# Two tables of places for a Mamba pipeline's work, laid anew, with a ninth buffer of h

## The chip, the core and the metric

One core of a Trainium2 chip runs the whole kernel in one launch. Every number is fp32. The metric is the device time of one execution in microseconds (us), the median of the runs.

## The reference

Four layers run one after the other on an image of 2 x 64 channels of 96 x 96 points. Layer 0 is attention over all 9216 points of a batch. Layer 3 is a 3 x 3 convolution whose taps come from the image's mean. The change concerns layers 1 and 2, which are Mamba blocks: a normalised input goes through a projection to 128 channels and a gate, a causal convolution of 4 taps, SiLU, and then a scan over the sequence with 16 states a channel:

```python
dt = softplus(dt_proj(x_proj(xc)[:4]) + dt_b)       # per channel and position
h  = exp(dt * A) * h + dt * B * xc                  # 128 channels x 16 states
y  = sum over states of h * C
out = out_proj((y + xc * D) * silu(gate))
```

Layer 1 scans the 9216 points of each batch as one sequence, so that its state is carried on. Layer 2 runs four such blocks, with RMS norms: forwards and backwards along the image's columns, then forwards and backwards along its rows. Its sequences are 96 long and start from nothing.

## The kernel before, in words

The Mamba work is cut into units of 768 positions: 24 in layer 1 (12 chunks of each batch) and 96 in layer 2 (8 sequences of 96, in pairs that share one normed input, one forwards, one backwards). A unit is 16 steps of 128 x 768: two halves of the positions (384 each), in each half two parts of eight states, in each part four steps of two blocks of 16 channels.

What one step does, and on which engine:

- `read` (L946): SP starts two transfers, which spread a block's rows of dt and of dt * xc from DRAM over 128 partitions. Six `spread` buffers hold them.
- `room` (L961) takes a buffer of h, of which there are `HELD` (8, L710), used in turn.
- `decay` (L967): ScalarE writes exp(dt * A), two activations of 384 columns (L973), into the h buffer.
- `shared` (L975): every fourth step TensorE makes B for four steps in one PSUM bank (L978). It must not overwrite a B that is still read.
- `inputs` (L984): VectorE multiplies the spread by B (L986) for two steps at a time, into the two PSUM tiles `place`.
- `scan` (L988): VectorE scans 768 columns (L1000; in layer 1 two scans of 384, L995) from decay and inputs into h. Then GpSimd multiplies h by C (L1002), which is called product below. In layer 1 it first copies the carried state (L996).
- `gather` (L1004): TensorE sums the products of a step into y (L1013), two steps at a time. After it the h buffer is free.

In some steps, the "asides" (`ASIDES`, L1154), the two operands change sides: GpSimd makes the inputs, into an SBUF tile `bx`, from a copy of B that ScalarE makes (`b_copy`, L980, line L982), and ScalarE puts the decay into `place`. Layer 1 has one aside a unit, at step 5; layer 2 has two, at steps 3 and 10, with a copy of B for each.

Beside the steps, parts of other units are done. The head of a unit runs two to three units ahead: the norm (`norm_centre` to `norm_affine`, L771 to L826; in layer 2 `image_0` and `image_1`, L790 and L795, copy the image and square it for both units of a pair), `conv` on TensorE (L830) and `conv_read` on ScalarE (L850), `gate_mm` and `gate_read`, `silu` (L859, with a table load before and after it), `step_mm` and `step_read` (L875, L876), `step_exp`, `step_log`, the sums on TensorE (`sum_mm`, L897) and `sum_read` (L902), `step_u` on GpSimd (L906), `step_write` on SP (L914), and `c_mm` with `c_read` (L920, L924) for C, twice. The end of a unit is done while the next one runs: `y_half` and `y_read` (L1017, L1020) take y from PSUM, `y_gate` (L1023) multiplies it by the gate on GpSimd, `tail_0` and `tail_1` (L1029) project it, and `tail_read` (L1043) writes the image. The matmuls' results of all these go through one PSUM tile, `mm`, so each waits for the reader of the one before. `other` prepares the next weights.

What sets the order: each of these has a place, a number of steps, in one of two tables, `CARRY` for layer 1 (L1056) and `FRESH` for layer 2 (L1104). `events` (L1160) adds the step's number to it, `run` (L1197) adds 16 for each unit and sorts everything of all units by place. In that order the instructions go into the queues of their engines. Each engine works its queue in order, and semaphores hold an instruction until what it needs is there. So a place matters only through the order that it gives on each engine.

Two rules of the built program are seen in the trace. Readers of one PSUM bank on two engines are ordered as well: where `b_copy` stands ahead of the inputs that read the same B, VectorE's instruction waits for ScalarE's copy. And `y_half` and `y_read` hold the first matmul of the next half of y.

Of the kernel before, what the change touches and what calls it, by code (L numbers as in the profile page):

```python
# [692 lines left out]
class Mamba:  # L693
# [13 lines left out]


    STEPS = 16
    HELD = 8  # L710
    BX = 1
    SPREADS = 6
    YG = 2
# [247 lines left out]
    def room(self, u, step):  # L961
        u.h[step] = self.by_half(self.work("h", bufs=self.HELD))
        u.decay[step], u.bx[step] = u.h[step], self.place(step)
        if step in self.aside(u):
            u.decay[step], u.bx[step] = self.place(step), self.by_half(self.work("bx", bufs=self.BX))
# [77 lines left out]
    def tail_read(self, u):  # L1043
# [10 lines left out]


    CARRY = dict(  # L1056
        norm_centre=-47.1,
        norm_square=-46.9,
        image_0=-37.15,
        image_1=-31.05,  # L1060
        norm_mean=-34.35,
        norm_root=-34.15,
        norm_scale=-32.6,
        norm_affine=-30.6,
        conv=-27.35,
        conv_read=-26.9,
        gate_mm=-26.15,
        gate_read=-24.85,
        silu=-24.6,
        step_mm=-23.9,  # L1070
        step_read=-23.1,
        step_exp=-22.05,
        step_log=-20.6,
        sum_mm_0=-20.23,
        sum_mm_1=-20.01,
        sum_read=-19.0,
        step_u=-12.65,
        step_write=-9.55,
        c_mm_0=-1.35,
        c_read_0=-0.05,  # L1080
        c_mm_1=1.65,
        c_read_1=2.45,
        y_half=11.97,
        y_read=18.72,
        y_gate=19.35,
        tail_0=25.55,
        tail_1=25.6,
        tail_read=26.05,
        other_0=2.77,
        other_1=4.25,  # L1090
        decay=-2.25,
        aside_decay=-0.75,
        aside=-1.7,
        inputs=0.0,
        scan=0.7,
        gather=3.65,
        shared=-1.8,
        read_0=-7.35,
        read_1=-3.25,
        read_2=-1.6,  # L1100
        read_3=0.5,
        b_copy_0=2.7,
    )
    FRESH = dict(  # L1104
        norm_centre=-47.0,
        norm_square=-41.9,
        image_0=-41.3,
        image_1=-36.9,
        norm_mean=-34.9,
        norm_root=-34.3,  # L1110
        norm_scale=-32.35,
        norm_affine=-30.75,
        conv=-27.35,
        conv_read=-26.4,
        gate_mm=-26.25,
        gate_read=-25.85,
        silu=-25.8,
        step_mm=-25.05,
        step_read=-24.5,
        step_exp=-22.6,  # L1120
        step_log=-21.4,
        sum_mm_0=-21.28,
        sum_mm_1=-21.16,
        sum_read=-19.5,
        step_u=-13.25,
        step_write=-9.35,
        c_mm_0=-1.5,
        c_read_0=-0.55,
        c_mm_1=1.65,
        c_read_1=2.75,  # L1130
        y_half=11.12,
        y_read=18.42,
        y_gate=18.65,
        tail_0=23.7,
        tail_1=24.6,
        tail_read=25.8,
        other_0=0.42,
        other_1=1.5,
        decay=-3.2,
        aside_decay=-1.15,  # L1140
        aside=-2.65,
        inputs=0.3,
        scan=0.7,
        gather=2.95,
        shared=-1.55,
        read_0=-8.2,
        read_1=-8.15,
        read_2=-5.7,
        read_3=-0.55,
        b_copy_0=-1.2,  # L1150
        b_copy_1=6.55,
    )
    TABLES = (CARRY, FRESH)
    ASIDES = ((5,), (3, 10))  # L1154
    CORE = ("decay", "aside_decay", "aside", "inputs", "scan", "gather", "shared", "read", "b_copy", "other")

    def aside(self, u):
        return self.ASIDES[bool(u.carry is None)]

# [422 lines left out]
```

## Time and profile before

| | us |
|---|---|
| median of 3 runs (lowest, highest) | 7484.11 (7477.61, 7490.45) |
| the profiled execution | 7481.5 |
| its span, first to last instruction | 7479.7 |
| layer 0 and the start of layer 1 (to 2553.5 us) | 2553.5 |
| layer 1 after its start (to 3569) | 1015.5 |
| layer 2 (to 7420) | 3851 |
| layer 3 | 59.7 |

Busy time in layer 2, as shares of its 3851 us: VectorE 97%, GpSimd 91%, ScalarE 84%, TensorE 77%. The granted TensorE clock was 0.93 on average there and 0.90 in layer 1.

Mean durations of the groups that the text uses, over the whole execution:

| line, engine | shape | count | mean ns |
|---|---|---|---|
| L1000 VectorE, scan | 128 x 768 | 1344 | 1736 |
| L1000 VectorE, scan in aside form | 128 x 768 | 192 | 1740 |
| L986 VectorE, inputs | 128 x 768 | 1704 | 948 |
| L1002 GpSimd, product | 128 x 768 | 1920 | 1818 |
| L986 GpSimd, aside's inputs | 128 x 768 | 216 | 1816 |
| L973 ScalarE, half a decay into h | 128 x 384 | 2688 | 607 |
| L982 ScalarE, copy of B | 128 x 384 | 216 | 469 |
| L859 ScalarE, SiLU | 128 x 1536 | 120 | 1483 |

How to read it: instructions of one engine overlap by about 0.1 us, so a pair takes less than twice the mean. An engine's idle time is put down to the instruction that ended last of those it waited for. What the kernel's time depends on is the idle time of the busiest engine in each stage, so a wait of another engine counts only as far as it reaches that one.

### The profile page before, as it was taken

Reading aid. Unit: us, or ns where it says so; the run is one execution under the profiler, and the core shown is the slowest. Engines: PE = TensorE matmul, PEld = TensorE weight load, DVE = VectorE, ACT = ScalarE, POOL = GpSimd, SP = SyncE. Lnnn points to the kernel's source line nnn. Section 1 sums busy time; section 2 is a strip of 40 time slices with the busy share of each in tenths; the row PEclk is TensorE's granted clock in tenths of the full one; section 3 lists DMA queues with packets and bytes.
Section 4 is the critical chain, followed back from the end, with each engine's and each line's share of the span. In section 5 each row is a group of like instructions: output and inputs, shape, how many; then the busy total and the mean of one; then the engine's idle time right before and its main releaser. Section 6 shows DMA issues by size and latency. Waiting matters only on the chain. (4 is left out here: it accounts for less than half of the span.)

```text
span 7479.7 us, 106202 instructions
## 1 busy us (share of the span) xinstructions
PE 6309.8 (84%) x38502; PEld 2338.3 (31%) x38502; DVE 6739.8 (90%) x5732; ACT 5470.8 (73%) x7876; POOL 4609.8 (62%) x3074
## 2 busy tenths in 40 slices
PE   9999999999998788787777777777777777777777
PEld 3333333333332232222222222222233233322322
DVE  6778877888886699999999999999999999999999
ACT  5555555555554687787888888888888888888884
POOL 0000000000000588888899898889999999999996
PEclk9999999999998799888999899989999999999998
DMA  1000000000000566566667666666667666666774
GB/s 46 1 1 1 1 1 1 3 5 5 6 6 29 129 167 156 150 168 155 169 175 184 165 180 169 175 168 181 178 174 183 178 179 180 175 180 177 180 183 127
DMA packets 301157, 878.12 MB, mean 117 GB/s; under 512 B 33608, under 2 KB 35660, under 8 KB 300112
## 3 DMA queue, kind: packets, MB, share of 16 engines
q1 hardware_dynamic: 300184, 869.94, 44.9%
q8 instruction: 304, 4.98, 0.3%
q14 instruction: 229, 1.88, 0.1%
q10 hardware_dynamic: 440, 1.32, 0.1%
HBM read 767.71 MB, written 103.42 MB: 116 GB/s over the span
## 5 line engine op out<-in xcount | busy, mean ns | idle before, releaser
L1002 POOL TENSOR_TENSOR h<-h,C 128x768 f32<-128x768 f32 x1920 | 3454.6, 1818 | 364.8 <-DVE h L1000 308.5
L1000 DVE TENSOR_TENSOR_SCAN h<-h,place 128x768 f32<-128x768 f32 x1344 | 2288.2, 1736 | 12.6
L313 ACT ACTIVATE e<-f_exp 128x1024 f32<-128x1024 f32 x1296 | 1257.7, 1022 | 986.8 <-PE f_exp L299 986.8
L986 DVE TENSOR_TENSOR place<-spread,B 128x768 f32<-128x768 f32 x1704 | 1548.2, 948 | 214.4 <-ACT xa L982 78.9
L973 ACT ACTIVATE h<-spread,xa 128x384 f32<-128x384 f32 x2688 | 1459.9, 607 | 80.9 <-PE y L1013 56.1
L324 PE MATMUL y<-e,xb 64*64 64x512 f32 x10368 | 1232.1, 590 | 0.0
L299 PE MATMUL f_exp<-theta,phi 64*64 64x512 f32 x10368 | 1229.9, 589 | 2.0 <-DVE xb L284 1.5
L1013 PE MATMUL y<-h,held 128*32 128x384 f32 x7680 | 1041.1, 532 | 212.3 <-POOL h L1002 212.3
L402 DVE TENSOR_TENSOR acc_e<-acc_e,e 128x1024 f32<-128x1024 f32 x612 | 771.7, 1261 | 300.9 <-ACT e L313 282.7
L338 POOL TENSOR_TENSOR ys<-ys,y_one 128x512 f32<-128x512 f32 x36 | 45.9, 1274 | 1456.8 <-DVE ys L337 1456.8
L411 DVE TENSOR_TENSOR acc_e<-acc_e,e 128x1024 f32<-128x1024 f32 x612 | 810.9, 1325 | 65.9 <-DVE acc_e L402 2.8
L978 PE MATMUL B<-raw,xa 128*128 128x384 f32 x960 | 497.6, 604 | 323.1 <-DVE place L986 310.4
L995 DVE TENSOR_TENSOR_SCAN h<-h,state,place 128x384 f32<-128x384 f32 x720 | 671.4, 992 | 1.7 <-PE y L1013 0.5
L324 PEld LDWEIGHTS y<-e,xb 64*64 64x64 f32 x10368 | 393.6, 133 | 728.2 <-issue 722.4
L299 PEld LDWEIGHTS f_exp<-theta,phi 64*64 64x64 f32 x10368 | 395.5, 133 | 715.0 <-issue 703.0
L363 POOL TENSOR_TENSOR xa<-xa,t_att 64x512 f32<-64x512 f32 x36 | 55.0, 1527 | 755.8 <-ACT t_att L361 735.2
L920 PE MATMUL mm<-raw,xa 128*128 128x384 f32 x960 | 386.4, 527 | 138.4 <-ACT C L924 78.2
L1013 PEld LDWEIGHTS y<-h,held 128*32 128x32 f32 x7680 | 198.7, 111 | 933.9 <-POOL h L1002 516.7
L743 PE MATMUL mm<-dtu,ident 128*128 128x384 f32 x960 | 418.2, 541 | 9.6 <-ACT xb L1048 4.9
L973 ACT ACTIVATE h<-spread,rates 128x384 f32<-128x384 f32 x720 | 394.9, 605 | 31.1 <-PE y L1013 16.8
L986 POOL TENSOR_TENSOR bx<-spread,xa 128x768 f32<-128x768 f32 x216 | 392.3, 1816 | 14.0 <-ACT xa L982 13.2
L973 ACT ACTIVATE place<-spread,xa 128x384 f32<-128x384 f32 x384 | 224.0, 583 | 199.8 <-DVE h L1000 193.3
(229 smaller groups left out, 7385.9 us busy)
## 6 DMA issues: line engine op xcount, KB each, us to landing
spread<-rows SPq DMA_DIRECT2D x1920, 384.0 KB, 6.1
rows<-dtu SPq DMA_DIRECT2D x120, 768.0 KB, 4.8
image<-pre SPq DMA_DIRECT2D x11, 384.0 KB, 2.3
xb<-image SPq DMA_DIRECT2D x11, 384.0 KB, 8.7
xa<-in_x SPq DMA_DIRECT2D x1, 2304.0 KB, 22.0
xa<-in_x SPq DMA_DIRECT2D x3, 384.0 KB, 11.5
xb<-in_x SPq DMA_DIRECT2D x3, 384.0 KB, 12.3
xa<-in_x SPq DMA_DIRECT2D x1, 1152.0 KB, 18.2
```

What stands on the lines that cost most here:

```text
L299: nc.tensor.matmul(f[rows_of(half), bass.ts(side, NB)], lhsT=phi[at, m * P + half * C : m * P + (half + 1) * C], rhs=theta[at, bass.ts(i, ...
L313: nc.scalar.activation(e, f, AF.Exp)
L324: nc.tensor.matmul(ys[half][rows_of(side)], lhsT=g[at, m, :], rhs=e[at, bass.ts(side, NB)], start=m < 2, stop=m >= KEYS - 2,)
L402: nc.vector.tensor_add(block.acc, block.acc, es[0])
L411: nc.vector.tensor_add(block.acc, block.acc, es[1])
L973: self.nc.scalar.activation(u.decay[step][:, q], dt[:, q], AF.Exp, scale=rate)
L978: self.nc.tensor.matmul(self.B, lhsT=u.w.bc[0][part], rhs=x, start=True, stop=True)
L986: engine.tensor_mul(u.bx[step], self.spread(u, step, 1), B)
L995: nc.vector.tensor_tensor_scan(h[:, q], decay[:, q], bx[:, q], state[:, q : q + 1], ALU.mult, ALU.add)
L1000: nc.vector.tensor_tensor_scan(*flat, 0.0, ALU.mult, ALU.add)
L1002: nc.gpsimd.tensor_mul(h, h, C)
L1013: self.nc.tensor.matmul(y, lhsT=self.t.gather[block // 4], rhs=u.h[step][:, q], start=False, stop=stop)
```

## The change

`HELD` goes from 8 to 9. Layer 1's aside goes from step 5 to step 3. Nearly all numbers of both tables are set anew. The code that uses them is the same. The diff, cut to the entries that alter an engine's order or that the text speaks of (layer 1 first):

```diff
-    HELD = 8
+    HELD = 9
...
     CARRY = dict(
...
-        norm_square=-46.9,
+        norm_square=-47.15,
...
-        norm_affine=-30.6,
+        norm_affine=-31.35,
...
-        gate_read=-24.85,
-        silu=-24.6,
-        step_mm=-23.9,
-        step_read=-23.1,
-        step_exp=-22.05,
-        step_log=-20.6,
+        gate_read=-25.25,
+        silu=-25.05,
+        step_mm=-24.7,
+        step_read=-23.55,
+        step_exp=-22.1,
+        step_log=-21.0,
...
-        step_u=-12.65,
-        step_write=-9.55,
-        c_mm_0=-1.35,
-        c_read_0=-0.05,
+        step_u=-12.15,
+        step_write=-8.3,
+        c_mm_0=-1.0,
+        c_read_0=0.05,
...
-        aside_decay=-0.75,
-        aside=-1.7,
+        aside_decay=-0.85,
+        aside=-1.8,
...
-        b_copy_0=2.7,
+        b_copy_0=0.2,
     )
     FRESH = dict(
...
-        norm_root=-34.3,
+        norm_root=-33.5,
...
-        step_log=-21.4,
+        step_log=-21.2,
...
-        c_read_0=-0.55,
-        c_mm_1=1.65,
+        c_read_0=-0.7,
+        c_mm_1=2.15,
...
-        y_half=11.12,
-        y_read=18.42,
-        y_gate=18.65,
-        tail_0=23.7,
-        tail_1=24.6,
+        y_half=10.72,
+        y_read=18.17,
+        y_gate=18.7,
+        tail_0=24.35,
+        tail_1=25.55,
...
-        decay=-3.2,
-        aside_decay=-1.15,
-        aside=-2.65,
-        inputs=0.3,
-        scan=0.7,
-        gather=2.95,
+        decay=-2.7,
+        aside_decay=-0.55,
+        aside=-2.3,
+        inputs=-0.05,
+        scan=0.8,
+        gather=3.05,
...
-        b_copy_0=-1.2,
-        b_copy_1=6.55,
+        b_copy_0=-1.05,
+        b_copy_1=7.45,
     )
-    ASIDES = ((5,), (3, 10))
+    ASIDES = ((3,), (3, 10))
```

Sorted within a unit's 16 steps, the queues of layer 2 differ in these places: on TensorE `c_mm_1` comes behind the gathers of steps 14 and 15 of the unit before, and `tail_0` behind those of steps 4 and 5; on ScalarE `c_read_0` comes ahead of decay 2, `y_read` ahead of decay 5, `y_half` ahead of `step_log` (it was behind `image_1`), and decay 1 ahead of `norm_root`. In layer 1, on ScalarE, `c_read_0`, `b_copy` and `norm_affine` open the unit, ahead of `norm_square`; decay 3 is an aside and decay 5 is not; `gate_read` comes ahead of decay 9 and `step_read` ahead of decay 11. On GpSimd the aside's inputs come behind product 0 (they were behind product 2), `y_gate` behind product 2 and `step_u` behind product 3. On TensorE `c_mm_0` comes behind the gathers of steps 10 and 11, and `norm_centre` ahead of those of steps 12 and 13.

More of the change, by code (lines that the diff above doesn't have):

```diff
@@ L1056 @@
     CARRY = dict(
-        norm_centre=-47.1,
-        norm_square=-46.9,
-        image_0=-37.15,
-        image_1=-31.05,
-        norm_mean=-34.35,
+        norm_centre=-47.35,
+        norm_square=-47.15,
+        image_0=-36.75,
+        image_1=-31.65,
+        norm_mean=-34.45,
         norm_root=-34.15,
         norm_scale=-32.6,
-        norm_affine=-30.6,
+        norm_affine=-31.35,
         conv=-27.35,
-        conv_read=-26.9,
-        gate_mm=-26.15,
-        gate_read=-24.85,
-        silu=-24.6,
-        step_mm=-23.9,
-        step_read=-23.1,
-        step_exp=-22.05,
-        step_log=-20.6,
-        sum_mm_0=-20.23,
-        sum_mm_1=-20.01,
-        sum_read=-19.0,
-        step_u=-12.65,
-        step_write=-9.55,
-        c_mm_0=-1.35,
-        c_read_0=-0.05,
-        c_mm_1=1.65,
+        conv_read=-27.15,
+        gate_mm=-26.45,
+        gate_read=-25.25,
[4 more added lines that the diff above has]
+        step_log=-21.0,
+        sum_mm_0=-20.63,
+        sum_mm_1=-20.21,
+        sum_read=-18.5,
+        step_u=-12.15,
+        step_write=-8.3,
+        c_mm_0=-1.0,
+        c_read_0=0.05,
+        c_mm_1=1.75,
         c_read_1=2.45,
@@ L1084 @@
         y_read=18.72,
-        y_gate=19.35,
-        tail_0=25.55,
+        y_gate=19.1,
+        tail_0=24.9,
         tail_1=25.6,
         tail_read=26.05,
-        other_0=2.77,
-        other_1=4.25,
+        other_0=2.87,
+        other_1=3.25,
         decay=-2.25,
-        aside_decay=-0.75,
-        aside=-1.7,
+        aside_decay=-0.85,
+        aside=-1.8,
         inputs=0.0,
@@ L1097 @@
         shared=-1.8,
-        read_0=-7.35,
+        read_0=-7.25,
         read_1=-3.25,
-        read_2=-1.6,
-        read_3=0.5,
-        b_copy_0=2.7,
+        read_2=-2.7,
+        read_3=0.35,
+        b_copy_0=0.2,
     )
     FRESH = dict(
[L1105 to L1109, printed above, removed]
-        norm_root=-34.3,
[L1111 to L1120, printed above, removed]
-        step_log=-21.4,
[L1122 to L1127, printed above, removed]
-        c_read_0=-0.55,
-        c_mm_1=1.65,
-        c_read_1=2.75,
-        y_half=11.12,
-        y_read=18.42,
-        y_gate=18.65,
-        tail_0=23.7,
-        tail_1=24.6,
@@ L1136 @@
-        tail_read=25.8,
-        other_0=0.42,
-        other_1=1.5,
-        decay=-3.2,
-        aside_decay=-1.15,
-        aside=-2.65,
-        inputs=0.3,
-        scan=0.7,
-        gather=2.95,
-        shared=-1.55,
[L1146 to L1149, printed above, removed]
-        b_copy_0=-1.2,
-        b_copy_1=6.55,
+        norm_centre=-46.85,
+        norm_square=-45.6,
+        image_0=-40.4,
+        image_1=-36.35,
+        norm_mean=-34.45,
+        norm_root=-33.5,
@@ new lines @@
+        norm_scale=-32.95,
+        norm_affine=-32.8,
+        conv=-27.2,
+        conv_read=-26.1,
+        gate_mm=-26.0,
+        gate_read=-25.6,
+        silu=-25.5,
+        step_mm=-25.25,
+        step_read=-23.75,
+        step_exp=-22.4,
+        step_log=-21.2,
+        sum_mm_0=-21.18,
+        sum_mm_1=-20.76,
+        sum_read=-19.0,
+        step_u=-12.6,
+        step_write=-10.75,
+        c_mm_0=-1.2,
+        c_read_0=-0.7,
+        c_mm_1=2.15,
+        c_read_1=2.85,
+        y_half=10.72,
@@ L1152 @@
+        y_read=18.17,
+        y_gate=18.7,
+        tail_0=24.35,
+        tail_1=25.55,
+        tail_read=25.8,
+        other_0=0.72,
+        other_1=0.4,
+        decay=-2.7,
[4 more added lines that the diff above has]
+        gather=3.05,
+        shared=-1.55,
+        read_0=-7.2,
+        read_1=-6.3,
+        read_2=-4.1,
+        read_3=-1.2,
+        b_copy_0=-1.05,
+        b_copy_1=7.45,
     )
     TABLES = (CARRY, FRESH)
-    ASIDES = ((5,), (3, 10))
+    ASIDES = ((3,), (3, 10))
```

## The prediction

> **What bounds the kernel now.** I read the engine totals, then the busy time by stage, then the waits of the long stage, then the timelines of single units.
>
> In the windows below (columns: stretch, its length, then busy us and count of PE, PEld, DVE, ACT, POOL, granted clock, DMA share, GB/s) the first row is layer 1 after its start, the second layer 2:
>
> ```profile
> 2553.50:3569.00 1015.50, 819.10 (x3210) 297.14 (x3208) 977.70 (x1101) 808.70 (x1251) 864.44 (x838) 0.90 0.63 160
> 3569.00:7420.00 3851.00, 2964.59 (x12626) 1131.00 (x12626) 3743.59 (x2920) 3230.13 (x5073) 3495.47 (x2059) 0.93 0.68 176
> ```
>
> VectorE is the bound: idle 37.8 us in layer 1 and 107.4 us in layer 2. No reordering can gain more than these 145 us. Layer 2 has 96 units of 16 steps, so it loses 1.12 us a unit. The waits between 4150 and 7300 us (78.5 units; us, times, longest) say to what:
>
> ```profile
> PE B L978 <- DVE place L986: 210.8, 145, 2.9
> PE y L1013 <- POOL h L1002: 156.2, 112, 2.7
> ACT raw L850 <- PE conv L845: 114.3, 72, 2.7
> DVE place L986 <- ACT xa L982: 64.8, 79, 1.9
> ACT h L973 <- PE y L1013: 45.8, 67, 1.0
> ```
>
> Only the fourth row is VectorE's: once a unit the inputs of step 0 or step 8 wait for ScalarE's copy of B (L982). The other rows show what makes that copy late. The timeline of two units, on three engines (start, us, engine, line, operation; in brackets the idle time before it and what ended it):
>
> ```profile
> 5243.10 0.91 PE L978 MATMUL B<-raw,xa 128*128 128x384 f32 x2 [1.97 <-DVE place L986]
> 5245.51 2.81 PE L845 MATMUL conv<-xn,xa 64*128 64x384 f32 x16
> ...
> 5260.75 0.84 PE L1013 MATMUL y<-h,held 128*32 128x384 f32 x4 [2.70 <-POOL h L1002]
> ...
> 5271.86 0.80 ACT L902 COPY dtu<-mm 128x768 f32<-128x768 f32 x1 [0.70 <-PE mm L743]
> 5273.34 1.12 ACT L973 ACTIVATE h<-spread,xa 128x384 f32<-128x384 f32 x2 [0.68 <-PE y L1013]
> ...
> 5277.52 1.83 DVE L986 TENSOR_TENSOR place<-spread,B 128x768 f32<-128x768 f32 x2 [1.56 <-ACT xa L982]
> ...
> 5322.35 0.91 PE L978 MATMUL B<-raw,xa 128*128 128x384 f32 x2 [2.13 <-DVE place L986]
> 5325.87 3.29 PE L845 MATMUL conv<-xn,xa 64*128 64x384 f32 x16
> ...
> 5336.60 1.83 DVE L986 TENSOR_TENSOR place<-spread,B 128x768 f32<-128x768 f32 x2 [0.74 <-ACT xa L982]
> ```
>
> After a pause of 2.13 us TensorE runs its convolution slowly; the convolution's reader, SiLU and the copy of B follow it in ScalarE's queue, and VectorE waits 0.74 us. After 1.97 us the convolution was fast and that wait is missing, but a second pause (2.70 us, for GpSimd's products) slows the sums, and the next copy is 1.56 us late. From 5196.67 to 5357.13 us (four units) VectorE waits 0.69 + 0.92 + 0.40 + 1.56 + 0.74 + 0.32 = 4.63 us. A unit without a wait takes 5277.52 - 1.56 - 5237.06 = 38.90 us.
>
> [...] The trace agrees: slow spells begin near 5203.5 and 5323.0 us[...]. It also shows the same 1.97 us pause both with and without a spell (5202.71 and 5243.10), so phase matters. [...] Here VectorE's reading at 5277.52 starts 0.03 us after ScalarE's copy of the same B ends, so a late copy holds VectorE though it needs nothing from it. [...] The scans stay at 1736 and 1740 ns whether the aside form or not, so moving the aside step changes no duration.
>
> **The change part by part.** The tables' figures act through the sort alone, so I sorted both tables and compared each engine's queue. In layer 2, VectorE's, GpSimd's and SP's queues are the same as before but for two small weight-preparing places; "half a step later" moves decays past nothing except the few entries named here.
>
> Ninth h buffer: decay 0 no longer needs the gathers of step 8 to be done. That removes the 0.68 us wait (45.8/67). It lies on the chain to step 0's copy only in the unit of each pair with the norm (every second unit), where the copy then ends near 5276.8 instead of 5277.5: 0.7 us.
>
> The second C product behind gathers 14 and 15 (they stood the other way round): gather 15 needs GpSimd's product of step 15, which ended 2.14 us after the start of the next unit's inputs (5239.20 against 5237.06). Then come gathers 0.85 and C product 1.5, done at +4.5 us; the inputs of step 2 end at +6.0 and release B for step 4. The pause is 1.5 us instead of 1.97 to 2.92[...], and the pause ahead of the gathers is 1.2 to 1.75. All lie under the 1.97 us that began a spell only sometimes, so I expect the convolution fast in nearly all units. It then ends 1.8 us after the start of the inputs of step 4 (5248.32 against 5246.50), not 3.4 (5329.16 against 5325.75). From its reader to the end of the copy for step 8 ScalarE needs 7.3 us, 9.2 in all, and the inputs of step 8 start at 10.0: the waits of 0.92, 0.74 and, following from them, 0.40 and 0.32 go. The 0.69 shrinks to 0.15, since from the reader to the next copy ScalarE has 27.7 us of work.
>
> What is late next: GpSimd's order is unchanged, so its pause of 2.5 to 2.7 us ahead of gathers 6 and 7 stays, and the sums stay slow: 0.70 (sum_read) + 0.15 = 0.85 us in every second unit, 48 x 0.85 = 41 us. Gain 107 - 41 = 66; I take 62, for units whose spell remains. Bounds: 100 us if the sums' spell goes too (48 x 0.15 remain), 17 us if the convolution stays slow as often as now (24 x 0.7).
>
> First tail half behind gathers 4 and 5: fills 0.85 of TensorE's 1.83 us wait for step_read; nothing on VectorE's path. Copy of C ahead of decay 2, y_read ahead of decay 5, y_half ahead of step_log, decay 1 ahead of the norm's root: nothing, covered by ScalarE's 1.45 us wait for scan 1 (place, 5242.22 and 5282.68). y_half delays step_log by 0.46 us, under the 0.7 us wait of sum_read at worst: up to 0.46 x 48 = 22 us if it isn't hidden.
>
> Layer 1, step_read ahead of decay 11: the inputs of step 12 wait for PE B once in most units, 25.1 us in 13 waits, because B stands behind the tails, which stand behind step_read:
>
> ```profile
> 3001.43 0.86 PE L743 MATMUL mm<-yg,mats 128*64 128x384 f32 x2 [2.68 <-ACT dtu L876]
> ...
> 3008.17 1.83 DVE L986 TENSOR_TENSOR place<-spread,B 128x768 f32<-128x768 f32 x2 [1.52 <-PE B L978]
> ```
>
> One decay (two activations) is 1.03 us: 13 x 1.03 = 13 us. At most all 25 go.
>
> Layer 1, aside at step 3 (GpSimd's product behind product 0, ahead of 1; step_u behind product 3): from the end of scan 14 GpSimd needs 9.6 us to have it (wait-free from product 14 on), VectorE reaches scan 3 after 10.0. The decay, now behind the copies of C and B, norm_affine, norm_square and decay 4, ends 8.4 us after the unit's start by my count, against 8.2. I take 1 us lost in all; bounds 0 and 24 x 0.5 = 12 us. The copy of B now waits for VectorE's inputs 0 and 1 (done at +1.8; ScalarE gets there at about +3): nothing. step_write follows step_u 1.25 steps later, at 7.7 of the unit's 16, and SP's reads keep their order behind it: with 4.8 us for the write and 6.1 for a spread (the page's medians; a step is 2.7 us) the next unit's first spread lands near 11.8, and its first decay comes at 13.75: nothing; without that cover each us late costs 24.
>
> Sum: 62 + 13 - 1 = 74 us off the profiled execution (span 7479.7, execution 7481.5): 7407.5. The median of the runs is 2.6 above that execution, so 7410.
>
> **The rivals.** *Phase decides (A):* [...] Then only the ninth buffer pays: 17 + 12 us, 7484 - 29 = 7455. For it: 1.97 us did and didn't trip. [...]
>
> *New wait (B), slower:* y_read now stands ahead of decay 5 and of step 3's decay, and waits for gather 15, so GpSimd's lag reaches VectorE's scan 3. With product 15 done at +L, that decay ends at L + 0.9 + 0.45 + 1.03 + 1.15 = L + 3.5; scan 3 starts at +7.8. At today's L of 2.14 there are 2.1 us to spare. From L = 4.3 each us costs 96 us; from 5.1 it outweighs the gain, and L = 5.3 gives about 7504. Against: GpSimd waits for scans 12 to 14 (1.45 us before each pair), so its lag is wiped out each unit.
>
> *Nothing happens (C):* ScalarE's chain is simply full, and removed waits reappear at the same copy: 7480. Against: it waits 114 us for the convolution, which shortens.
>
> **How the numbers follow.** Forecast 0.58 (7372 to 7440: the gain of 100 in layer 2 with 12 in layer 1 at the low end; y_half's 22 us and half of layer 1's 12 lost at the high end: 7438). A 0.20 (7440 to 7466). C 0.07. B 0.12. Below 7372 0.03. The range 7372 to 7466 holds 0.78. A measurement tells about 0.2%, 15 us, from no change: faster (under 7469) 0.80, same 0.08, slower 0.12.
>
> **What would show it.** Right: the row "DVE place L986 <- ACT xa L982" falls to about half; "ACT raw L850 <- PE conv L845" falls to about 0.9 us each; "ACT h L973 <- PE y L1013" vanishes; PE's waits before B for step 4 stay under 1.8 us; VectorE idles about 45 us in layer 2 and 26 in layer 1. Wrong: convolutions of 3.3 us as often as now (A); "DVE h L1000 <- ACT place L973" or "POOL bx" growing to over 50 us (B); or VectorE's idle time unchanged with other names (C).

## The result and the profile after

The kernel after takes 7397.73 us (median of 4 runs, 7391.99 to 7400.75), the kernel before 7487.28 beside it: a ratio of 0.9879 with a 95% interval of 0.9862 to 0.9896. That is 90 us off, where the prediction said 74 (7410) and a range of 7372 to 7466. The profiled execution of after has a span of 7389.9 us, of before 7479.7.

By stage, from first scan to first scan (L995, L1000): layer 1 took 1117.0 us and takes 1094.3, layer 2 took 3848.0 to its last scan and takes 3784.2. So layer 2 gave 63.8 (predicted 62) and layer 1 gave 22.7 (predicted 12). The start gave 2.8, which the other runs with layer 1's new table do not repeat (their first scan comes at 2453.4 to 2458.2 us, that of before at 2454.9).

How far can one execution be trusted? The runs below that keep the old table of layer 1 took 1108.5 to 1124.7 us there, and those that have the new one 1093.6 to 1099.4. In layer 2 the old table took 3844.6 to 3850.1. So a difference between two single traces shows little where it is under some 16 us in layer 1 or 6 us in layer 2.

The windows of layer 1 after its start and of layer 2 in the kernel after (same columns as before):

```profile
2552.00:3546.00 994.00, 805.19 (x3192) 291.69 (x3192) 972.34 (x1097) 806.82 (x1249) 862.54 (x833) 0.91 0.63 162
3546.00:7332.00 3786.00, 2999.17 (x12626) 1153.43 (x12625) 3730.78 (x2917) 3234.11 (x5067) 3495.70 (x2058) 0.95 0.69 179
```

VectorE now idles 21.7 us in layer 1 (it was 37.8; 26 predicted) and 55.2 in layer 2 (107.4; 45 predicted). Its work in layer 2 fell too, from 3743.6 to 3730.8 us, which nothing in the prediction foresaw and no run explains. The waits of 79.4 units of layer 2 in the kernel after (us, times, longest):

```profile
PE y L1013 <- POOL h L1002: 296.0, 246, 2.7
PE B L978 <- DVE place L986: 151.7, 158, 4.1
ACT raw L850 <- PE conv L845: 120.2, 79, 4.1
DVE place L986 <- ACT xa L982: 32.0, 40, 2.0
```

VectorE's wait for the copy of B has fallen to half, from 64.8 us to 32.0, and the row of decay 0 (ACT h L973 <- PE y L1013) is gone. TensorE's pauses in the first two rows have not shrunk in sum: they moved from B (210.8 to 151.7) to the gathers (156.2 to 296.0). What they do to the convolution has changed. The timeline shows 94 of layer 2's convolutions as one group of 16 matmuls in each run. Of these, 27 took over 2.95 us before (called slow from here on), and 2 take it now.

The timeline of one unit with the norm in the kernel after, on TensorE, ScalarE and VectorE (columns as before):

```profile
5651.81 0.91 PE L978 MATMUL B<-raw,xa 128*128 128x384 f32 x2 [1.43 <-DVE place L986]
...
5654.15 2.81 PE L845 MATMUL conv<-xn,xa 64*128 64x384 f32 x16
...
5669.54 0.84 PE L1013 MATMUL y<-h,held 128*32 128x384 f32 x4 [2.71 <-POOL h L1002]
5671.48 1.62 PE L978 MATMUL B<-raw,xa 128*128 128x384 f32 x2 [1.10 <-DVE place L986]
5672.89 1.49 PE L743 MATMUL mm<-dtu,ident 128*128 128x384 f32 x2
...
5678.46 0.81 PE L743 MATMUL mm<-kept,ident 128*128 128x384 f32 x2
...
5680.59 0.80 ACT L902 COPY dtu<-mm 128x768 f32<-128x768 f32 x1 [2.28 <-PE mm L743]
5681.29 2.13 ACT L973 ACTIVATE h<-spread,xa 128x384 f32<-128x384 f32 x4
5683.32 0.88 ACT L807 ACTIVATE xa<-mm,eps 128x768 f32<-128x768 f32 x1
5684.24 0.84 ACT L808 ACTIVATE xa<-xa 128x768 f32<-128x768 f32 x1
5684.99 0.46 ACT L982 COPY xa<-B 128x384 f32<-128x384 f32 x1
5685.48 1.83 DVE L986 TENSOR_TENSOR place<-spread,B 128x768 f32<-128x768 f32 x2 [0.81 <-ACT xa L982]
```

B comes after a pause of 1.43 us and the convolution behind it is fast, as predicted. The pause of 2.71 us ahead of gathers 6 and 7 is still there, the sums behind it are slow (1.49 us a pair of matmuls at a mean granted clock of 0.57 from 5672.8 to 5678.4 us, then 0.81 at 1.00), `sum_read` waits 2.28 us for them, and the copy of B for step 0 comes 0.81 us late. That is the 0.85 us in every second unit that the prediction left over. In the whole of layer 2 it is 47 waits, 34.9 us.

In layer 1, VectorE's inputs (L986) waited 25.1 us for TensorE's B. The group's row in the kernel after (columns: line, engine, operation, shapes and count | busy us, mean ns of one | idle us before it and what ended most of it):

```profile
L986 DVE TENSOR_TENSOR place<-spread,B 128x768 f32<-128x768 f32 x340 | 306.5, 943 | 5.9 <-PE B L978 4.4 <-ACT xa L982 1.4
```

Of that wait 4.4 us are left. In the runs that keep the old table it is 21.6 to 33.0.

### The profile page after: what moved, and what is told of

The parts are those of the page before. It is cut to its first block, busy times and chain, and to the rows that moved or that the text cites. A ratio compares the mean times of both kernels' runs of the same rounds, so it can differ in the third digit from the quotient of the medians.

```text
span 7389.9 us, 106037 instructions
## 1 busy us (share of the span) xinstructions
PE 6327.8 (86%) x38502; PEld 2353.7 (32%) x38502; DVE 6725.5 (91%) x5732; ACT 5478.5 (74%) x7876; POOL 4613.1 (62%) x3074
## 5 line engine op out<-in xcount | busy, mean ns | idle before, releaser
L1000 DVE TENSOR_TENSOR_SCAN h<-h,place 128x768 f32<-128x768 f32 x1344 | 2285.9, 1736 | 13.3 <-ACT place L973 0.5
L986 DVE TENSOR_TENSOR place<-spread,B 128x768 f32<-128x768 f32 x1704 | 1545.4, 946 | 130.5 <-PE B L978 90.5
L973 ACT ACTIVATE h<-spread,xa 128x384 f32<-128x384 f32 x2688 | 1445.9, 605 | 8.5 <-DMA spread<-rows 7.1
L1013 PE MATMUL y<-h,held 128*32 128x384 f32 x7680 | 1105.5, 515 | 372.0 <-POOL h L1002 371.2
L978 PE MATMUL B<-raw,xa 128*128 128x384 f32 x960 | 492.5, 598 | 269.9 <-DVE place L986 267.2
L995 DVE TENSOR_TENSOR_SCAN h<-h,state,place 128x384 f32<-128x384 f32 x720 | 670.6, 990 | 2.4
L1013 PEld LDWEIGHTS y<-h,held 128*32 128x32 f32 x7680 | 212.2, 109 | 1140.8 <-POOL h L1002 741.5
L986 POOL TENSOR_TENSOR bx<-spread,xa 128x768 f32<-128x768 f32 x216 | 393.0, 1819 | 5.5 <-ACT xa L982 3.5
L973 ACT ACTIVATE h<-spread,rates 128x384 f32<-128x384 f32 x720 | 393.1, 606 | 3.5 <-DMA spread<-rows 2.9
L978 PEld LDWEIGHTS B<-raw,xa 128*128 128x128 f32 x960 | 159.4, 208 | 585.7 <-DVE place L986 419.2
```

Source lines behind the costliest of these rows:

```text
L973: self.nc.scalar.activation(u.decay[step][:, q], dt[:, q], AF.Exp, scale=rate)
L978: self.nc.tensor.matmul(self.B, lhsT=u.w.bc[0][part], rhs=x, start=True, stop=True)
L986: engine.tensor_mul(u.bx[step], self.spread(u, step, 1), B)
L995: nc.vector.tensor_tensor_scan(h[:, q], decay[:, q], bx[:, q], state[:, q : q + 1], ALU.mult, ALU.add)
L1000: nc.vector.tensor_tensor_scan(*flat, 0.0, ALU.mult, ALU.add)
L1013: self.nc.tensor.matmul(y, lhsT=self.t.gather[block // 4], rhs=u.h[step][:, q], start=False, stop=stop)
```

## The experiments

The theory, at the start: two moves make the gain, a ninth buffer that frees decay 0 and `c_mm_1` that shortens the pause ahead of B, and in layer 1 `step_read`. The rivals: that the buffer does it all, that the rest of the table does, that phase alone decides. "Layer 2" below is the time from its first scan to its last in the profiled run; the kernel before has 3848.0 and the kernel after 3784.2 there. All ratios are to the kernel before, with their 95% intervals.

**The ninth buffer alone**, in the kernel before.

```diff
-    HELD = 8
+    HELD = 9
```

> The kernel before with nine buffers of h alone. Theory (two causes in layer 2: ScalarE's decay 0 waiting for the gathers of step 8, and TensorE's slow spell in the convolution): the decays' waits for PE y, 45.8 us between 4150 and 7300 us, vanish, but this reaches VectorE only in the norm's units whose convolution is fast, about 24 x 0.7 = 17 us: 0.2% faster, the convolutions slow as often as before. Rival (the buffer is the whole of layer 2's gain): 64 us faster, 0.9%.

Measured: 7471.93 us, ratio 0.9983 (0.9975 to 0.9992), 12 us off. But layer 2 is only 3.1 us shorter in the trace (3844.9), no more than the same table differs from run to run. Layer 1 is 7.0 us shorter (1110.0), and that too is within its spread: with nine buffers and the same table of layer 1 the run with both moves, below, took 1124.7 there. So where the 12 us lie isn't shown. In layer 2 VectorE idles 106.7 us (107.4 before), and 26 of 94 convolutions are slow. The wait of decay 0 is gone, yet VectorE's row stands at 63.1 us (64.8 before): the copy of B comes as late as before. The total was near the expected 17, but not by the expected way.

**The second C product alone**, in layer 2's table of the kernel before.

```diff
-        c_mm_1=1.65,
+        c_mm_1=2.2,
```

> The kernel before with the second product for C behind the gathers of steps 14 and 15 in layer 2, alone (c_mm_1 at 2.2). Theory: the pause ahead of B for step 4 falls below 1.8 us, nearly all convolutions take 2.8 us, and VectorE no longer waits at the copy for step 8; with eight buffers each pair still loses 1.56 us at the other copy, 48 x 1.56 = 75 us of the 107: 32 us faster, 0.4%. Rival ([...]not the length of the pause): no change, and slow convolutions as often as before.

Measured: 7427.91, ratio 0.9921 (0.9907 to 0.9934). Layer 2 takes 3797.5 us, 50.5 less, where the theory expected far less. Slow convolutions: 3 of 94. So this one number makes most of layer 2's gain, without the buffer. The rows of the waits in this run:

```profile
ACT h L973 <- PE y L1013: 47.9, 71, 0.7
DVE place L986 <- ACT xa L982: 35.8, 42, 1.6
```

Decay 0 still waits for its buffer, 71 times, and VectorE's wait is down all the same. Nor does a pause slow the convolution by its length alone. In the same run one unit has its pause ahead of the gathers, longer than the 1.97 us of before, and its convolution is fast:

```profile
5182.10 1.20 PE L1013 MATMUL y<-h,held 128*32 128x384 f32 x4 [2.43 <-POOL h L1002]
5183.23 2.84 PE L920 MATMUL mm<-raw,xa 128*128 128x384 f32 x4
5185.91 0.81 PE L978 MATMUL B<-raw,xa 128*128 128x384 f32 x2
...
5188.18 2.82 PE L845 MATMUL conv<-xn,xa 64*128 64x384 f32 x16
```

The gather (1.20 us instead of 0.84) and the C product (2.84 for four matmuls that take 1.45 at 5176.79) pay for the pause; at 5185.91 TensorE is fast again (0.81 us for the two matmuls of B). In this unit the move has put the slow stretch on the C product, which VectorE's path doesn't wait for, and left the convolution out of it. In other units it splits the pause, 0.65 us ahead of the gathers and 1.48 ahead of B (conv at 5148.0, 2.81 us).

The kernel before has long pauses with a fast convolution, too. This one is longer than any that the prediction shows there:

```profile
5800.87 1.23 PE L978 MATMUL B<-raw,xa 128*128 128x384 f32 x2 [2.91 <-DVE place L986]
5801.90 1.49 PE L1008 MATMUL y<-raw,xa 128*128 128x384 f32 x2
5803.31 1.51 PE L1013 MATMUL y<-h,held 128*32 128x384 f32 x8
5804.75 2.81 PE L845 MATMUL conv<-xn,xa 64*128 64x384 f32 x16
```

B and the sums of y are slow here (a mean granted clock of 0.57 from 5800.8 to 5804.8 us), and the convolution begins when that is over (1.00). At 5724.62, after 2.92 us, it took 3.59. The two are told apart in the last section.

**Both**, in the kernel before.

```diff
-    HELD = 8
+    HELD = 9
...
-        c_mm_1=1.65,
+        c_mm_1=2.2,
```

> The kernel before with both: nine buffers of h, and the second product for C behind gathers 14 and 15. Theory: together they leave 0.85 us a pair, so they give nearly all of layer 2's gain: 60 us faster (more than the sum of the two alone, 17 + 32), VectorE's wait for ScalarE's copy in layer 2 about 40 us. Rival (the other swaps in layer 2's queues, the first tail half or the reading of y, carry a part): clearly less than 60, down to 30.

Measured: 7432.1, ratio 0.9926 (0.9912 to 0.9940); layer 2 takes 3793.8. The total is near the theory's, but the buffer adds nothing that the runs can tell (0.9921 without it).

**Layer 1's table alone.** The kernel before with the whole new `CARRY` table (the diff shows one entry of it) and the aside at step 3, nothing new in layer 2.

```diff
     CARRY = dict(
...
-        step_read=-23.1,
+        step_read=-23.55,
...
     )
-    ASIDES = ((5,), (3, 10))
+    ASIDES = ((3,), (3, 10))
```

> The kernel before with layer 1's new table and its aside at step 3, eight buffers and layer 2 as before. Theory: VectorE's waits for PE B in layer 1 (25 us) go, and the start gains 3: 22 to 26 us faster, 0.3%. Rival (layer 1's gain needs the ninth buffer as well, since decay 0 waits 0.67 us there too): under 12 us.

Measured: 7459.61, ratio 0.9967 (0.9955 to 0.9979), 25 us off, as the theory said: layer 1's gain does not need the ninth buffer. Layer 1 takes 1093.6 us, as in the kernel after (1094.3).

**`step_read` ahead of decay 11, alone**, in layer 1's table of the kernel before.

```diff
-        step_read=-23.1,
+        step_read=-23.3,
```

> The kernel before with one number changed: layer 1's step_read at -23.3, so that it stands ahead of decay 11 in ScalarE's queue. Theory (the tails, and B for step 12 behind them, wait for step_read): B comes 1.03 us earlier and more where the tails then run at full clock, so the 25.1 us of VectorE's waits for PE B fall by 13 to 22: 13 to 22 us faster, 0.2 to 0.3%. Rival (the aside's move from step 5 to step 3, or gate_read ahead of decay 9, makes the gain in layer 1): under 6 us.

Measured: 7464.12, ratio 0.9964 (0.9951 to 0.9978), 22 us off by the medians. Its profiled run shows 12.7 us less in layer 1 (1104.3), and the inputs' wait for TensorE's B halved, from 25.1 us:

```profile
L986 DVE TENSOR_TENSOR place<-spread,B 128x768 f32<-128x768 f32 x341 | 308.1, 945 | 18.6 <-PE B L978 13.2 <-DMA spread<-rows 2.7 <-ACT xa L982 2.3
```

The prediction's 13 us for this step agree with the trace, but a single trace is not enough: the interval of the runs is 16 to 37. Over all runs, layer 1 took 1116.8 us on average with the old table (five runs, 1108.5 to 1124.7), 1103.0 with this one number changed (two, 1104.3 and 1101.7) and 1096.2 with the new table (seven). That puts some 14 us on `step_read` and some 7 on the rest of the table.

**The C product put back**, ahead of gathers 14 and 15, all else as after.

```diff
-        c_mm_1=2.15,
+        c_mm_1=2.0,
```

> The changed kernel with the second product for C put back ahead of the gathers of steps 14 and 15 in layer 2 (c_mm_1 at 2.0). Theory: slow convolutions are back in half of the units and VectorE waits at the copy for step 8 again: 30 to 50 us slower than the changed kernel, so 40 to 60 faster than the one before. Rival[...]: as fast as the changed kernel.

Measured: 7420.83, ratio 0.9907 (0.9892 to 0.9922), 23 us above after by the medians, where 30 to 50 were expected. Layer 2 takes 3814.2, 30 more than after; 14 of 94 convolutions are slow, not half. This is the puzzle of the set: the move alone gave 50.5, everything but the move gives 33.8 (of which the buffer 3.1), and together they give 63.8. Something pays about 31 us where `c_mm_1` stands as before, and about 10 where it is moved: one of the swaps that the prediction costed at nothing, or the times at which the pauses fall. The second is not ruled out, for TensorE pauses 1.8 us or more ahead of the convolution's B as often as in the kernel before (63 of 94 times, before 66), and only 14 of these convolutions are slow, not 27.

**Eight buffers**, all else as after.

```diff
-    HELD = 9
+    HELD = 8
```

> The changed kernel with eight buffers of h. Theory: decay 0 waits 0.7 us for the gathers of step 8 again, on the chain to the copy in every second unit: 48 x 0.7 = 34 us slower than the changed kernel. Rival (the buffer does nothing once the convolution is fast): equal to the changed kernel.

Measured: 7404.55, ratio 0.9889 (0.9873 to 0.9904); layer 2 takes 3788.7, 4.5 more than after. Decay 0 waits again (46.5 us, 69 times in the window of 3130 us), and VectorE's row stays at 32.9 us. The theory's 34 us were wrong: the medians differ by 7 us, within the intervals.

**The aside of step 10 behind product 7.** GpSimd makes the inputs of step 10 between products 6 and 7; here it makes them one product later, to take away the pause of 2.7 us.

```diff
-                add(s + table["aside"], "inputs", s, self.nc.gpsimd)
+                add(s + table["aside"] + (0.15 if s == 10 else 0), "inputs", s, self.nc.gpsimd)
```

> The changed kernel with GpSimd's inputs for step 10 one place later, behind the product of step 7 instead of ahead of it. Theory (what is left, 0.8 us a pair, comes from TensorE's pause of 2.7 us ahead of gathers 6 and 7, which slows the sums): the pause shrinks to about 0.9 us, the sums run at full clock and VectorE's wait at the copy falls from 35 us in layer 2 to under 15: 20 to 35 us faster than the changed kernel. Rival (new wait): the bx of step 10 comes 1.8 us later and VectorE's scan 10 waits for it, up to 96 x 1.0 us: slower.

Measured: 7397.74, ratio 0.9881 (0.9866 to 0.9896): no change. TensorE's timeline of this run tells why:

```profile
5669.65 0.84 PE L1013 MATMUL y<-h,held 128*32 128x384 f32 x4 [0.92 <-POOL h L1002]
5671.44 0.84 PE L1013 MATMUL y<-h,held 128*32 128x384 f32 x4 [0.95 <-POOL h L1002]
5675.15 1.62 PE L978 MATMUL B<-raw,xa 128*128 128x384 f32 x2 [2.87 <-DVE place L986]
5676.56 1.49 PE L743 MATMUL mm<-dtu,ident 128*128 128x384 f32 x2
```

The pause ahead of the gathers fell from 2.71 to 0.95 us, and the next one, ahead of B, grew from 1.10 to 2.87. B waits until VectorE has read the old one, whatever GpSimd does. The removed pause came back at the next wait and the sums are as slow as before.

**`sum_read` behind decay 0.** If the sums stay slow (1.49 us a pair), ScalarE need not stand still for them. The kernel after, layer 2's table:

```diff
-        sum_read=-19.0,
+        sum_read=-18.5,
```

> The kernel after, with one number: in layer 2 sum_read half a step later (-19.0 to -18.5), so that ScalarE computes decay 0 of the next unit before it reads the sums, not after. What is left of layer 2's idle time in the kernel after is 47 waits of VectorE for the copy of B, 0.74 us each, 34.9 us, one per pair of units; in that unit ScalarE stands 2.28 us at the sums (L902) with decays 0 and 1 queued behind it. Theory (ScalarE's queue is what makes that copy late, not TensorE's slow clock itself): decay 0 fills 1.03 us of the 2.28, but the norm's root then waits for the mean (L765 ends at 5682.8, root would start at 5682.4), so the copy comes 0.47 us earlier, not 1.03; about 20 of the 35 us go: 7378 against 7398. Rival 1: the slow sums themselves are the limit, and the copy waits for TensorE's B behind them: nothing changes, 7398. Rival 2: decay 0 waits for something that the sums had covered (its h buffer, needed by gather 7, or its rows): slower than 7398.

Measured: 7388.16, ratio 0.9877 (0.9862 to 0.9892). By the trace it is a little better than after: layer 2 takes 3776.3 us, VectorE idles 43.2, and its wait for the copy falls from 32.0 us to this:

```profile
ACT h L973 <- PE y L1013: 37.8, 56, 0.7
DVE place L986 <- ACT xa L982: 16.1, 36, 1.9
```

So the order of ScalarE's queue made about half of that wait, with the sums no faster. But part of what the move freed is lost again: now decay 1 waits for its buffer (the first row), which the wait for the sums had covered. The ratios of this run and of after differ by less than their intervals, so it isn't shown to be faster.

**The norm's root behind the copy of B, as well**, on top of the last edit.

```diff
-        norm_root=-33.5,
-        norm_scale=-32.95,
+        norm_root=-32.95,
+        norm_scale=-32.65,
```

> The run with sum_read at -18.5, and the norm's root (two activations, 1.7 us) behind the copy of B for step 0 (norm_root -33.5 to -32.95, norm_scale -32.95 to -32.65, GpSimd's order unchanged). Theory: the copy of B then waits only for TensorE's B (done near 5684.4 in the unit at 5680, where it is needed by 5684.7), so nearly all of the 35 us of waits in layer 2 go: 7365, at least 7372. Rival 1: the root's lateness reaches GpSimd's scale of the norm and through it the convolution: the 0.4 to 0.8 us waits come back at the copy for step 8, 7385 to 7400. Rival 2: as with the sum alone, TensorE's B is what is late: 7398.

Measured: 7424.57, ratio 0.9924 (0.9911 to 0.9938), 27 us above after by the medians, 34 by the ratios, and worse than the first rival said. Waits in its layer 2:

```profile
PE mm L920 <- ACT xa L807: 63.0, 46, 1.4
...
DVE place L986 <- ACT xa L982: 29.4, 38, 1.7
DVE xa L671 <- PE mm L569: 15.3, 8, 2.0
```

The root (L807) reads the PSUM tile `mm`. Read later, it holds the C product behind it (first row). VectorE's waits in preparing weights (L671 and others, most for matmuls of L569 that share the tile) come to 36 us, and its wait for the copy of B is back: at 5663.66 us, ahead of step 8, it is 0.99. The mean granted clock of this run, 0.961, is the highest of all; it is slower all the same.

**Two numbers.** If two moves are the change, they should add. The kernel before, one entry of each table:

```diff
-        step_read=-23.1,
+        step_read=-23.3,
...
-        c_mm_1=1.65,
+        c_mm_1=2.2,
```

> The kernel before with two numbers of the change only: c_mm_1 of layer 2 from 1.65 to 2.2 and step_read of layer 1 from -23.1 to -23.3. Alone they gave 59 us and 22 us off. Theory (these two moves are the change; buffers, aside step and the other hundred figures give nothing): the gains add, 7484 - 59 - 22 = 7403, within 8 us of the kernel after. Rival (the rest of the table carries a part that the single runs did not show, above all in layer 2, where the kernel after idles 55 us and the run with c_mm_1 alone 66): 7410 to 7420.

Measured: 7414.09, ratio 0.9908 (0.9895 to 0.9922): 67 us off, three quarters of the change's 90. The rival was right: the rest of the change carries about 20 us, 7.4 in layer 1 and 12.8 in layer 2 by the traces (1101.7 and 3797.0).

**One of the swaps costed at nothing: the copy of C ahead of decay 2.** The kernel before with nine buffers, and in layer 2's table:

```diff
-        c_read_0=-0.55,
+        c_read_0=-1.195,
```

> The kernel before with nine buffers of h, and one number: in layer 2 the copy of the first C product (c_read_0) from -0.55 to -1.195, so that it stands ahead of decay 2 and behind the copy of B, as in the changed table. Why: with c_mm_1 put back ahead of gathers 14 and 15, the changed table still took 34 us off layer 2, while nine buffers alone took 3; so some of the small swaps that I had costed at nothing pay 31 us when c_mm_1 is not moved. In the run with nine buffers TensorE's second C product waits 1.32 us for this copy in every second unit (5264.30), and then 1.97 us for B of step 4. Theory 1 (this copy is the swap that pays; the shorter first pause keeps TensorE's clock up): the row of PE's wait for the copy of C falls from 45 us to under 10, slow convolutions from 25 of 92 to about 14, time 7441. Theory 2 (it only moves the pause: the C product and gathers 14 and 15 end 1 us earlier, so the pause ahead of B of step 4 grows from 1.97 to 3.0 us and starts a slow spell in nearly every such unit; what pays in the changed table is another swap, one that splits the pause by holding gather 15 for GpSimd): slow convolutions 40 or more of 92, time 7480 to 7495. Theory 3 (pauses add up the same, nothing changes): 7472.

Measured: 7496.53, ratio 1.0018 (1.0011 to 1.0026), 15 us slower than before and some 25 slower than nine buffers alone. TensorE's wait for this copy fell from 45.0 us to 8.5, and layer 2 took 24 us more than in the run with nine buffers. Its window of layer 2:

```profile
3566.00:7435.00 3869.00, 3027.43 (x12626) 1148.22 (x12626) 3740.48 (x2916) 3228.46 (x5067) 3496.64 (x2057) 0.92 0.67 175
```

VectorE idles 128.5 us, 22 more than with nine buffers, and 33 of 94 convolutions are slow, not 26 (the second theory said 40 or more). In this unit the first pause is short and the second long:

```profile
5281.86 1.56 PE L920 MATMUL mm<-raw,xa 128*128 128x384 f32 x4 [0.31 <-ACT C L924]
5283.35 1.74 PE L1013 MATMUL y<-h,held 128*32 128x384 f32 x8
5287.18 0.91 PE L978 MATMUL B<-raw,xa 128*128 128x384 f32 x2 [2.09 <-DVE place L986]
```

Taking a wait from TensorE made the kernel slower. In this unit what it no longer idles there it idles just ahead of B and the convolution. In sum that isn't shown: TensorE's waits ahead of B are 219.4 us here and 216.0 with nine buffers alone, and pauses of 1.8 us or more ahead of the convolution's B are as frequent (70 and 68 of 94). More of them end in a slow convolution, so the times at which they fall are a rival reading. By itself this swap is not what pays in the run with the C product put back. Whether another one does (`tail_0`, `y_read`, `y_half`, or decay 1 ahead of the root) was not tried, and stays open.

## Why the prediction was right, point by point

- **What bounds it:** right. VectorE's idle time went down in both layers by 16 and 52 us, and in layer 2 the wait that changes most is the one for the copy of B.
- **The second C product, convolution fast:** right in kind, too small in its share. The step gave it what was left after the buffer; alone it gives 50.5 us of layer 2. The foreseen pause of 1.5 us ahead of B is there: 1.43 us in the timeline above, and 0.66 us in the other unit of the pair. That such pauses leave the convolution fast held without exception (894 of 894, last section). The test by length was half of the matter: a pause of 2.43 us was harmless to the convolution when a C product stood between, and in the kernel before most of the pauses of 1.97 us and more were harmless, too (39 of 64). The lower bound of 17 us, convolutions as slow as before, did not occur.
- **The ninth buffer:** wrong. "It lies on the chain to step 0's copy only in the unit of each pair with the norm", 24 to 48 times 0.7 us, was 17 to 34 us. Layer 2 shows 3.1 (alone), 3.7 (on top of the C product) and 4.5 (taken from the kernel after), each within the spread of single traces. The wait of decay 0 went as foreseen; that it lies on the chain to the copy was the mistake. Rival A's 7455 built on the same term.
- **Sums stay slow, 41 us left:** right, 34.9 measured. The remaining 20 us of idle time are small gaps and waits for prepared weights.
- **The row "ACT raw L850 <- PE conv L845":** wrong. It was to fall to 0.9 us each and is 1.5 (120.2 over 79; 1.6 before). The convolution ends earlier; why ScalarE still waits as long for it was not traced. The wait for the copy of B halved all the same, so this row was no measure of it.
- **The swaps at nothing:** wrong in sum. With the rest of `FRESH` layer 2 is about 10 us shorter beside the C product and 31 without it, and with one swap by itself the kernel took 25 us more. Which swap does it, and by which wait, is not known.
- **Layer 1:** `step_read` was right: 13 us foreseen, some 14 measured. The net of 12 was too small, for the rest of the table with the aside at step 3, to which I gave a loss of 1 us, gives some 7. In the first 100 us of the layer VectorE is busy 61.8 us after and 57.5 before, so some of it lies there.
- **The rivals:** B's rows did not grow: VectorE waited 0.5 us for an aside's decay (DVE h L1000 <- ACT place L973) in all of layer 2. C is refuted by the time. A's 7455 is refuted, too: the C product's move, not the buffer, makes layer 2's gain, and it keeps the convolution fast wherever the pause falls. But phase goes a long way to tell which of the longer pauses have a slow convolution behind them, as the last section shows.

That the total came within 12 us is in part luck, because errors had opposite signs: the buffer was taken too large, the C product and the small moves too small.

## What to carry to other kernels

Where a pause of one engine slows its next work (here a convolution of 3.29 us instead of 2.81), look for a place in the queue that splits the pause, as the C product did here. Where it can't be split, ask what the next work is: put work that nobody waits for behind the pause, and what the bound engine waits for behind that. A wait removed from an engine that is not the bound is worth nothing until its next wait has been named; here three such removals gave 0, a few us, or a loss. Compare stages of single traces only after seeing how far the same code differs from run to run. And a sum that comes out right doesn't prove its terms: run each alone, and take each away from the whole.

## What the hardware showed that I had not expected

A pause's length doesn't decide alone whether the convolution behind it is slow. The runs show how length and time go together. For each of the 94 convolutions, take TensorE's pause ahead of the last B before it (L978):

| run | pause under 1.8 us | slow | 1.8 us or more | slow |
|---|---|---|---|---|
| before | 28 | 0 | 66 | 27 |
| nine buffers alone | 26 | 0 | 68 | 26 |
| copy of C ahead of decay 2 | 24 | 0 | 70 | 33 |
| C product put back | 31 | 0 | 63 | 14 |
| second C product alone | 91 | 0 | 3 | 3 |
| after | 92 | 0 | 2 | 2 |

In all fourteen traces, no convolution behind a pause under 1.8 us is slow (894 of them); the shortest pause with a slow one behind it is 1.84 us. So the move of the C product works by making these pauses short.

Whether a convolution behind a longer pause is slow goes by when it starts. The trace records TensorE's granted clock, which is 1.00 or 0.50 in these two kernels. In the kernel before there are 288 stretches of one clock, and their starts lie on one grid: whole multiples of 3.4133 us apart, each within 0.001 us. The 192 of the kernel after give 3.4133 us as well. Of the 106 stretches at 0.50 in layer 2 before, 51 last 3.41 us, 52 last 6.83 and three are longer. So the slow convolution at 5325.87 us lies in part in a stretch at 0.50 (5323.46 to 5326.87), and at 5245.51, where it is fast, the clock is 1.00 throughout. In the kernel before each of the 27 slow convolutions overlaps such stretches by 0.39 us or more, and of the 67 others none by more than 0.27. Why the clock changes at these times and no others the traces don't show.

Lay the convolutions of the kernel before on a grid of this period, from the first instruction on. Of the 66 behind a longer pause, 28 start between 0.10 and 0.50 of a period, and 27 of these are slow. The other 38 start between 0.55 and 0.95, and none is slow. The six traces with many long pauses (the first four rows and the two runs that change only layer 1) have 401 such convolutions. For each trace one stretch of the period was chosen that best parts slow from fast, and 396 of the 401 fall on the right side. With periods of 3.40 or 3.42 us instead, the best stretches get 270 and 273 right, with 3.412 or 3.414 us 370 and 383; calling all of them fast would get 248. So of these periods the one of the clock's records fits the convolutions best.

The short pauses need no such luck: in the run with the second C product alone, 44 convolutions come behind pauses of 1.35 to 1.5 us, in every tenth of the period, and none is slow.

The grid also fits the way in which slow convolutions took turns in the kernel before. A pair of units took 80.2 us there (the convolutions at 5165.3 and 5245.5), which is 23.5 of these periods: of those after a pause of 1.97 to 2.13 us, the ones at 5165.3 and 5325.9 us took 3.37 and 3.29, those at 5245.5 and 5405.9 took 2.81. From 5844.9 us on, slow convolutions of this kind (5844.89, 6083.79, 6322.70) came every third pair, 238.9 us or 70.0 periods apart. In the kernel after a pair takes 78.5 us, 23.0 periods, and from 5600 to 6000 us the same wait of 0.8 us comes once in each pair. No run was made to change the ratio of a pair's time to this period alone, so what it is worth in time, in the C product put back above all, stays open.
